# A two-layer graph kernel on Trainium2: a sixth residual-row buffer, a closing norm in four steps, and instructions held to their place

## The chip, the cores and the metric

The kernel runs on one core of one Trainium2 chip. The metric is device time in microseconds (us). Below, PE is the tensor engine (PEld its weight loads), DVE the vector engine, ACT the scalar engine, POOL the GpSimd engine and SP the engine that issues most of the plain DMAs. L1295 is line 1295 of the kernel before.

## The reference, cut to what matters

The input is 32 graphs of 512 nodes with 256 numbers each, and a 0/1 adjacency matrix of each graph. Two layers follow each other. Layer 0 is message passing over the adjacency and a large feed-forward network of sorted (max and min) lines; the change doesn't touch it. Layer 1 is attention over the graph's edges and then a token mixer:

```
attention of one graph, x of 512 x 256:
  h      = layernorm(x) W                      4 heads of 64
  att    = exp(leaky(own + other)) * adjacency, normalised over the neighbours
  v      = relu(att h + bias) + h
  v      = (v - mean) * (var + eps)^-0.5 * gamma + beta     per head: the closing norm
  x      = x + v
mixer of the same graph:
  s      = softmax(layernorm(x) W_slice)       8 heads x 64 slices: "sw"
  tokens = s^T layernorm(x) / sum(s)           "yTp"
  tokens -> gated scan of 64 steps (projection, short convolution, decay matrix, norm)
  x      = x + s (tokens W_out)                "outp"
  out    = x
```

## The kernel before, in words

Layer 1 is `layer1_plain` (L866). It runs two streams over the same engines. The stream `attentions` (L1300) does, graph after graph, `prepare(b + 1)` woven with `attention(b)` and then the closing norm `norm(b, av)`. The stream `mixer(g)` (L1564) takes two graphs at a time (GB = 2, so 16 groups): `slices` for each of them (L1306), `tokens` (L1351), `scan` (L1376) and `unslice` (L1554), which adds outp into x and stores the graph on SP's queue (L1562).

**Order.** Both streams are Python generators. Each `yield n` of the mixer gives the attention stream n times PACE steps to emit; PACE comes from TURNS, STEPS and WANTED, the planned numbers of steps. That decides in which order instructions are handed to the framework's scheduler, which then orders each engine's instructions by priority; `tc.keep_in_program_order` holds one instruction to its handed place. PSUM has four buffers of the kind "any" (hp, lgp, yTp, xp, yp, outp and others) and four of the kind "pv" (avp, adp and the transposes back).

**prepare(b)** (L1135 to 1192) waits, in the planner, until graph b - AHEAD_X is stored, because the tile x has AHEAD_X = 5 buffers. Then POOL gathers the graph's rows by four indirect DMAs (L1142), SP transposes the mask (L1091), POOL issues the narrowing copy of a later mask (`shorten`, L1085). DVE takes the statistics of each row (L1114, 1115), POOL their pow (L31), ACT normalises (L1121), PE transposes (L1130, x3T), and four tiles hp are multiplied on PE (L1171). From each hp tile ACT makes the exponentials hv, mine and other (L1174, 1177, 1178) and the copy ht (L1179), DVE the values hv times the exponential (L1175, read from PSUM). minep (L1183) is the transpose of mine, which goes out to DRAM and comes back broadcast as own (L1187, L1190).

**attention(b)** (L1206): DVE makes the weighed edges att (L1201), PE the sums avp (L1237) and adp (L1242), one row of 16 + 8 matmuls for each of four node tiles; then transposes back (dp, bp, L1220), the division (L1265) and a row of biases added by a DMA (av<-added, L953). `norm` is then put in the list `unfinished` and is stepped from inside the next graph's attention loop.

**norm(b, av)** (L1272): DVE relu and add (L1282), mean (L1284, 1285), subtract (L1286); ACT square (L1288); a first yield; DVE sum of squares (L1290, 1291), POOL pow (L1292), DVE times gamma (L1293); a second yield; DVE times the pow (L1295), DVE add into x (L1296).

**slices** (L1306): statistics d of x, normalise, transpose (x4T), lgp (L1327), ACT exponential (L1328), DVE times a bias factor (L1329), sum, reciprocal and division (L1332 to 1334), PE yTp (L1339) and the transposes swp (L1344). **scan**: xp (L1392), bcp, dtp, zp (L1385), the convolutions on DVE (L1409, 1411), gp (L1479), segp (L1483), qp (L1493), mix (L1500 to 1502), yp (L1509), y (L1512 to 1514), yTp<-ident,y (L1519), oTp (L1527), the mean square msp (L1535), rms on DVE (L1538) and its pow on POOL (L1539), vp (L1549), v (L1551).

Of the kernel before, what the change touches and what calls it, by code (L numbers as in the profile page):

```python
# [13 lines left out]
AF = mybir.ActivationFunctionType  # L14
ALU = mybir.AluOpType
AX = mybir.AxisListType
# [3 lines left out]
P = 128  # L20
N = 512
D = 256
NT = N // P
DC = D // P
LN_EPS = 1e-5
# [839 lines left out]
def layer1_plain(tc, ident, eps, x2s, ranks, adj, w, out, over, ps):  # L865
# [3 lines left out]
    nc = tc.nc  # L869
    B = adj.shape[0]  # L870
    SEG = B // len(x2s)
    GB = 2
    AH, _, HO = w["W"].shape
# [5 lines left out]
    DI = H * C  # L879
# [6 lines left out]
    SLOPE = 0.01  # L886
    HE = HO + 1
    AP = AH // 2
    TURNS = AP * NT + 6
    STEPS = 11  # L890
    WANTED = 68
    AHEAD = 3
    ATT = 2 * (AHEAD + 2) + AP + 1
    HW = P // AH
    AHEAD_X = 2 * GB + 1
    PACE = 1.04 * GB * (TURNS + STEPS) / WANTED

    SMALL = 30.0 * 30.0 / D
# [2 lines left out]
    with ExitStack() as ctx:  # L901
# [11 lines left out]
        def psum(tag, name):  # L913
            return ps.tile([P, N], F32, tag=tag, name=name)
# [36 lines left out]
        def add_rows(dst, i):  # L951

            nc.gpsimd.dma_start(dst, added[i].partition_broadcast(P), accum_op=ALU.add)  # L953
# [44 lines left out]
        with tc.tile_pool(name="raw", bufs=2, side="right") as raw:  # L998
# [67 lines left out]
            for c in range(DC):  # L1066
                sq = raw.tile([P, H * G], F32, tag="wsl2", name=f"wsl2_{c}")
# [68 lines left out]
        def prepare(b):  # L1136

            while b >= AHEAD_X and b - AHEAD_X not in stored:
                yield True
            xt = xs[b] = sb.tile([P, NT, D], F32, tag="x", name=f"x{b}", bufs=AHEAD_X)  # L1140
            for t in range(NT):
                nc.gpsimd.indirect_dma_start(  # L1142
                    out=xt[:, t, :], out_offset=None, in_=x2s[b // SEG],
                    in_offset=bass.IndirectOffsetOnAxis(
                        ap=ranks[:, b * NT + t : b * NT + t + 1].bitcast(U32), axis=0))

            hv = sb.tile([P, NT, AH, HE], F32, tag="hv", name=f"hv{b}")
            xn = hv.rearrange("p t h e -> p (t h e)")[:, : NT * D].rearrange("p (t d) -> p t d", t=NT)
            if b:
                turn(b)  # L1150
            shorten(b + 2)
            yield
            yield
            yield
            normed(xt, xn, f"c{b}")
            add_rows(xt.rearrange("p t d -> p (t d)"), BETA)
            yield
            mask = masked.pop(b)
            xnT = yield from turned(xn, "x3T", f"x3T{b}")
            yield  # L1160


            ht = sb.tile([P, NT, AH * HO], F32, tag="ht", name=f"ht{b}")
            nc.scalar.activation(ht.rearrange("p t e -> p (t e)").bitcast(BF16), mask.rearrange("p t n -> p (t n)"),
                                 AF.Square, bias=centre, accum_out=edges[:, b : b + 1])
            other = sb.tile([P, NT, AH], F32, tag="other", name=f"other{b}")
            mine = sb.tile([P, AH, NT], F32, tag="mine", name=f"mine{b}")
            for t in range(NT):
                ph = psum("any", f"hp{b}_{t}")
                for c in range(DC):  # L1170
                    nc.tensor.matmul(ph[:, : AH * (HO + 2)], xnT[:, c, t * P : (t + 1) * P], wa[:, c, :],  # L1171
                                     start=c == 0, stop=c == DC - 1)
                d = ph[:, AH * HO : AH * HO + AH]
                nc.scalar.activation(hv[:, t, :, HO], d, AF.Exp)  # L1174
                nc.vector.tensor_mul(hv[:, t, :, :HO], ph[:, : AH * HO].rearrange("p (h e) -> p h e", h=AH),  # L1175
                                     hv[:, t, :, HO:].to_broadcast([P, AH, HO]))
                nc.scalar.activation(mine[:, :, t], ph[:, AH * (HO + 1) : AH * (HO + 2)], AF.Exp, scale=1.0 - SLOPE)
                nc.scalar.activation(other[:, t, :], d, AF.Exp, scale=SLOPE - 1.0)
                nc.scalar.copy(ht[:, t, :], ph[:, : AH * HO])  # L1179
                yield  # L1180

            pt = psum("any", f"minep{b}")
            nc.tensor.transpose(pt[: AH * NT, :P], mine.rearrange("p h t -> p (h t)"), ident)  # L1183
            row = sb.tile([AH * NT, P], F32, tag="turned", name=f"turned{b}", bufs=1)
            nc.scalar.copy(row, pt[: AH * NT, :P])
            own_row = dr.tile([AH, N], F32, tag="own", name=f"ownd{b}")
            nc.sync.dma_start(own_row.rearrange("h (t p) -> (h t) p", p=P), row)  # L1187
            own = [wide("own", f"own{b}_{h}", AH + 1) for h in range(AH)]
            for h in range(AH):
                nc.sync.dma_start(own[h], own_row[h].partition_broadcast(P))  # L1190
            ready[b] = mask, ht, hv, other, own
            yield
# [11 lines left out]
        def attention(b):  # L1204

            mask, ht, hv, other, own = ready[b]  # L1206
# [19 lines left out]
            for i, (q, j) in enumerate(turns):  # L1226
                if i + AHEAD < len(turns):
                    begin(b, i + AHEAD)
                elif b + 1 in ready:
                    begin(b + 1, i + AHEAD - len(turns))  # L1230

                if q + 1 == AP:
                    ends = dict(start=j == 0, stop=j == NT - 1)
                    for p in range(AP):
                        for k in range(2 * HO // HW):
                            h, e = 2 * p + k * HW // HO, k * HW % HO
                            nc.tensor.matmul(pv[p][k * HW : (k + 1) * HW, :], hv[:, j, h, e : e + HW],  # L1237
                                             weighed[b, h, j], **ends)
                    if j == 0:
                        pd = psum("pv", f"adp{b}")  # L1240
                    for h in range(AH):
                        nc.tensor.matmul(pd[h * HW : (h + 1) * HW, :], hv[:, j, h, HO:].to_broadcast([P, HW]),  # L1242
                                         weighed.pop((b, h, j)), **ends)
                yield
                if unfinished and i not in (0, 3):
                    next(unfinished[0], None)
                    yield
                    if i > 3:
                        unfinished.pop()
# [12 lines left out]
            for q in range(AP):  # L1262
                bt = back(vT[q], f"bp{q}_")
                heads = slice(2 * q, 2 * q + 2)
# [7 lines left out]
        unfinished = []  # L1272

        def norm(b, av):

            _, ht, _, _, _ = ready[b]
            xt = xs[b]
            NG = NT * AH
            flat = av.rearrange("p t h e -> p (t h e)")
            rows = av.rearrange("p t h e -> p t (h e)")  # L1280
            heads = av.rearrange("p t h e -> p (t h) e")
            nc.vector.scalar_tensor_tensor(flat, flat, 0.0, ht.rearrange("p t e -> p (t e)"), ALU.max, ALU.add)  # L1282
            mu = sb.tile([P, 2, NG], F32, tag="mu", name=f"mu{b}")
            nc.vector.tensor_reduce(mu[:, 0, :], heads, AX.X, ALU.add)  # L1284
            nc.vector.tensor_scalar_mul(mu[:, 0, :], mu[:, 0, :], 1.0 / HO)
            nc.vector.tensor_sub(heads, heads, mu[:, 0, :].unsqueeze(2).to_broadcast([P, NG, HO]))  # L1286
            sq = ht.rearrange("p t (h e) -> p (t h) e", e=HO)
            nc.scalar.activation(sq, heads, AF.Square)  # L1288
            yield
            nc.vector.tensor_reduce(mu[:, 1, :], sq, AX.X, ALU.add)  # L1290
            nc.vector.tensor_scalar(mu[:, 1, :], mu[:, 1, :], 1.0 / HO, 1e-6, ALU.mult, ALU.add)
            nc.gpsimd.tensor_tensor(mu[:, 1, :], mu[:, 1, :], eps[:, 1:2].to_broadcast([P, NG]), ALU.pow)  # L1292
            nc.vector.tensor_mul(rows, rows, gamma.unsqueeze(1).to_broadcast([P, NT, AH * HO]))  # L1293
            yield
            nc.vector.tensor_mul(heads, heads, mu[:, 1, :].unsqueeze(2).to_broadcast([P, NG, HO]))  # L1295
            nc.vector.tensor_add(xt, xt, rows)  # L1296
            del ready[b]
            attended.add(b)

        def attentions():  # L1300
            yield from prepare(0)
            for b in range(B):
                nxt = prepare(b + 1) if b + 1 < B else iter(())
                yield from woven(attention(b), TURNS - 4, nxt, STEPS)
            for _ in unfinished[0]:
# [69 lines left out]
        def scan(g, uT):  # L1375
# [50 lines left out]
            v, e, u, r, dt = (sp[:, i, :] for i in range(5))  # L1426
# [59 lines left out]
            pt = psum("any", f"xtp{g}")  # L1486
# [30 lines left out]
            pt = psum("any", f"yTp{g}")  # L1517
# [14 lines left out]
            pm = psum("any", f"msp{g}")  # L1532
# [2 lines left out]
                    nc.tensor.matmul(pm[i * G : (i + 1) * G, j : j + 1], ident[:, j * G : (j + 1) * G], ms,  # L1535
                                     start=True, stop=True)
            rms = sb.tile([P, GB], F32, tag="rms", name=f"rms{g}")
            nc.vector.tensor_scalar(rms, pm[:, :GB], 1.0 / DI, LN_EPS, ALU.mult, ALU.add)  # L1538
            nc.gpsimd.tensor_tensor(rms, rms, eps[:, 1:2].to_broadcast([P, GB]), ALU.pow)  # L1539
            yield 2  # L1540

# [689 lines left out]
```

## Time and profile before

| what | value |
|---|---|
| runs of the kernel | 4503.5, 4513.17, 4514.52 us (median 4513.17) |
| profiled execution, whole | 4515.02 us |
| its span | 4513.3 us |
| mean granted clock of PE | 0.94 |
| layer 1 within the span | from about 2395 us to the end |
| start of outp in four groups that follow each other | 2715.20, 2844.05, 2973.26, 3102.16 us |
| last stretch, from the 15th group's outp to the end | 124.00 us |

The profile is of one execution. Its page gives busy times of engines over the whole span; the trace can be cut into stretches. A chain of waits is read from the end backwards: each piece is the work that released the next one. A wait is given as engine and line that waited, engine and line that released it, the sum in us, the number of waits and the longest. In a timeline line the bracket at the end is the idle time of that engine before the instruction, and who ended it. "issue" is time for which the trace shows no wait. The granted clock is 1.00 at full speed.

### The profile page before, as it was taken

What the parts mean: (1) busy time and instruction counts of PE and PEld (TensorE: products, weight loads), DVE (VectorE), ACT (ScalarE), POOL (GpSimd) and SP (SyncE); (2) the same over time, 40 slices, a digit from 0 to 9 for tenths busy, and PEclk for the clock granted to TensorE, in tenths of its full rate; (3) what the DMA queues carried; (4) which work ended last, traced back from release to release, by engine and by line L of the source; (5) the groups of instructions that cost most, each with busy time, mean ns of one, the idle gap of its engine ahead of it and who ended that gap; (6) DMA issues with size and microseconds to landing.
All of it is one profiled execution on the core that took longest, in us unless ns stands there. A gap on an engine that the chain in (4) does not pass through costs nothing.

```text
span 4513.3 us, 56135 instructions
## 1 busy us (share of the span) xinstructions
PE 3933.4 (87%) x19799; PEld 2468.0 (55%) x19799; DVE 3204.0 (71%) x6909; ACT 2198.0 (49%) x4305; POOL 1570.2 (35%) x2069
## 2 busy tenths in 40 slices
PE   5567898899988999889997999898998898989987
PEld 4454565656656656555553555555555455555555
DVE  6678888897788877867765766656666666666663
ACT  3345565556565665545663444344444443444433
POOL 2356544664446554444313122222211222222110
PEclk8778999999999999989998999999999999999998
DMA  5546543664446643564315233333322333333210
GB/s 129 160 142 224 184 140 110 206 202 154 135 129 206 194 141 109 169 216 160 129 59 117 52 76 79 80 80 68 83 68 62 73 80 80 80 70 76 62 38 20
DMA packets 301248, 524.04 MB, mean 116 GB/s; under 512 B 104823, under 2 KB 180227, under 8 KB 300956
## 3 DMA queue, kind: packets, MB, share of 16 engines
q0 software_dynamic: 117120, 383.06, 30.6%
q1 hardware_dynamic: 183836, 137.30, 10.4%
q8 instruction: 158, 2.59, 0.2%
q14 instruction: 134, 1.10, 0.1%
HBM read 463.11 MB, written 73.95 MB: 119 GB/s over the span
## 4 chain that ended last, share of the span: by engine, by line
PE 32%; DVE 31%; DMA 15%; issue 9%; POOL 8%; ACT 4%; SPq 1%; DVEq 0%; POOLq 0%; ACTq 0%
DVE acc L637 4%; PE clsp L623 4%; PE po L652 4%; DMA av<-added 3%; PE yTp L1339 3%; PE gatep L623 3%; PE outp L1559 3%; POOL mu L1292 2%; DMA rows<-table,xs 2%; DMA out<-x 2%; DMA rows<-table,tops 2%; DVE best L598 2%; PE oTp L1527 2%; DVE att L1201 2%; PE avp L1237 2%
## 5 line engine op out<-in xcount | busy, mean ns | idle before, releaser
L623 PE MATMUL clsp<-xnT,wc 128*128 128x512 f32 x1024 | 524.8, 631 | 46.7 <-ACT cls L625 34.4
L623 PE MATMUL gatep<-xnT,wg 128*128 128x512 f32 x1024 | 496.8, 605 | 9.3 <-ACT gate L625 9.3
L652 PE MATMUL po<-wd,acc 128*128 128x256 f32 x2048 | 457.3, 382 | 8.4 <-DVE acc L641 5.9
L652 PEld LDWEIGHTS po<-wd,acc 128*128 128x128 f32 x2048 | 389.2, 192 | 75.2 <-issue 9.6
L1201 DVE SCALAR_TENSOR_TENSOR att<-own,other,mask 128x512 f32<-128x512 f32 x512 | 358.3, 737 | 12.8 <-DMA own<-ownd 12.8
L598 DVE SCALAR_TENSOR_TENSOR best<-rows,xs,best 128x1024 f32<-128x1024 f32 x212 | 272.6, 1288 | 126.8 <-ACT best L592 79.5
L637 DVE SCALAR_TENSOR_TENSOR acc<-past,fld,acc 128x512 f32<-128x512 f32 x448 | 344.6, 772 | 23.8 <-ACT past L636 16.0
L1237 PE MATMUL avp<-att,hv 128*32 128x512 f32 x2048 | 333.0, 601 | 7.2 <-DVE att L1201 7.2
L1339 PE MATMUL yTp<-sw,x 128*128 128x512 f32 x512 | 262.1, 666 | 88.0 <-DVE sw L1334 88.0
L623 PEld LDWEIGHTS gatep<-xnT,wg 128*128 128x128 f32 x1024 | 196.8, 196 | 253.3 <-issue 203.5
L632 ACT ACTIVATE acc<-tz,fld 128x512 f32<-128x512 f32 x256 | 198.7, 776 | 279.1 <-PE tz L630 247.4
L636 ACT ACTIVATE past<-tz,fld 128x512 f32<-128x512 f32 x448 | 291.5, 693 | 79.3 <-DVE acc L637 77.7
L595 POOL DMA_INDIRECT rows<-table,xs x212 | 251.5, 1186 | 170.3 <-DVE best L598 117.3
L623 PEld LDWEIGHTS clsp<-xnT,wc 128*128 128x128 f32 x1024 | 183.9, 200 | 185.9 <-issue 114.1
L434 PE MATMUL pm<-h,adj 128*128 128x258 f32 (+1 forms) x1024 | 182.9, 326 | 103.9 <-DVE keep L427 42.6
L1327 PE MATMUL lgp<-wsl,x4T 128*128 128x512 f32 x512 | 241.3, 617 | 22.4 <-ACT x4T L1131 22.4
L625 ACT ACTIVATE gate<-gatep,fld 128x512 f32<-128x512 f32 x256 | 175.4, 685 | 146.4 <-PE gatep L623 124.0
L553 POOL DMA_INDIRECT xs<-rows_of,order x128 | 156.7, 1225 | 215.3 <-DVE acc L637 93.3
L1339 PEld LDWEIGHTS yTp<-sw,x 128*128 128x128 f32 x512 | 104.9, 214 | 227.5 <-DVE sw L1334 126.2
L1559 PE MATMUL outp<-v,swT 128*128 128x256 f32 x1024 | 226.2, 379 | 0.0
L434 PEld LDWEIGHTS pm<-h,adj 128*128 128x128 f32 x1024 | 152.8, 215 | 129.2 <-issue 73.4
L625 ACT ACTIVATE cls<-clsp,fld 128x512 f32<-128x512 f32 x256 | 176.0, 687 | 95.3 <-PE clsp L623 58.8
(593 smaller groups left out, 8550.7 us busy)
## 6 DMA issues: line engine op xcount, KB each, us to landing
adj<-in_adj POOLq DMA_DIRECT2D x128, 256.0 KB
x<-added POOLq DMA_DIRECT2D x64, 512.0 KB
own<-ownd SPq DMA_DIRECT2D x128, 256.0 KB
rows_of<-keep SPq DMA_DIRECT2D x32, 550.0 KB
x<-in_x SPq DMA_DIRECT2D x32, 512.0 KB
x2s<-xs SPq DMA_DIRECT2D x32, 512.0 KB
short<-in_adj POOLq DMA_DIRECT2D x32, 512.0 KB
av<-added POOLq DMA_DIRECT2D x32, 512.0 KB
```

The lines of the kernel that those rows point to most:

```text
L434: nc.tensor.matmul(pm[:, : c1 - c0], a[:, i, t * P : (t + 1) * P], h[:, i, c0:c1], start=i + c0 == 0, stop=i + 1 == NT and c0 > 0)
L595: nc.gpsimd.indirect_dma_start(out=row, out_offset=None, in_=table, in_offset=bass.IndirectOffsetOnAxis(ap=idxs[:, k : k + 1].bitcast(U32) ...
L598: nc.vector.scalar_tensor_tensor(m, row, vals[:, k : k + 1], m, ALU.add, ALU.max)
L623: nc.tensor.matmul(pf, wf[:, c, f * P : (f + 1) * P], xnT[:, c, :], start=c == 0, stop=c == DC - 1)
L625: nc.scalar.activation(o, pf, fn, bias=fld[:, f, bf : bf + 1], scale=1.0 if fn == AF.Gelu else 0.5)
L636: nc.scalar.activation(r, z, AF.Relu, bias=fld[:, f, AT + b : AT + b + 1])
L637: nc.vector.scalar_tensor_tensor(y, r, fld[:, f, CH + b : CH + b + 1], y, ALU.mult, ALU.add)
L652: nc.tensor.matmul(po[:, i, :], acc[f][:, t * P : (t + 1) * P], wd[:, f, :], start=f == 0, stop=f == FC - 1)
L1201: nc.vector.scalar_tensor_tensor(e, own[h], other[:, j, h : h + 1], mask[:, j, :], ALU.max, ALU.mult)
L1237: nc.tensor.matmul(pv[p][k * HW : (k + 1) * HW, :], hv[:, j, h, e : e + HW], weighed[b, h, j], **ends)
L1339: nc.tensor.matmul(py, xn[:, t, c * P : (c + 1) * P], sw[:, t, :], start=t == 0, stop=t == NT - 1)
L1559: nc.tensor.matmul(po[:, :D], swT[:, k, t * P : (t + 1) * P], v[:, k, :], start=k == 0, stop=k == KC - 1)
```

## The change

Six things are edited, all in layer 1.

1. AHEAD_X goes from 5 to 6: one more buffer of the tile x. TURNS goes from 14 to 15 and WANTED from 68 to 69, so that PACE goes from 0.765 to 0.784.
2. In `prepare` the values multiply becomes a function `values(t)`, which reads the copy ht in SBUF in place of the PSUM tile and is handed over one tile later.
3. minep is kept in program order.
4. `unfinished` is stepped at the turns 1, 2, 3 and 6 of the attention loop's eight; before it was stepped at 1, 2 and from 4 on.
5. `norm` has two more yields and so four steps: ahead of the square and ahead of the sum of squares. Its relu, square, sum of squares and the multiply by the pow are kept in program order.
6. In `scan` there is a `yield 1` ahead of rms, and rms is kept in program order.

The narrowing copy was kept in program order already; with the six of the points 3, 5 and 6 that makes seven.

```diff
-    TURNS = AP * NT + 6
+    TURNS = AP * NT + 7
     STEPS = 11
-    WANTED = 68
+    WANTED = 69
...
-    AHEAD_X = 2 * GB + 1
+    AHEAD_X = 2 * GB + 2
...
+            def values(t):
+                nc.vector.tensor_mul(hv[:, t, :, :HO], ht[:, t, :].rearrange("p (h e) -> p h e", h=AH),
+                                     hv[:, t, :, HO:].to_broadcast([P, AH, HO]))
+
             for t in range(NT):
...
                 nc.scalar.activation(hv[:, t, :, HO], d, AF.Exp)
-                nc.vector.tensor_mul(hv[:, t, :, :HO], ph[:, : AH * HO].rearrange("p (h e) -> p h e", h=AH),
-                                     hv[:, t, :, HO:].to_broadcast([P, AH, HO]))
...
                 nc.scalar.copy(ht[:, t, :], ph[:, : AH * HO])
+                if t:
+                    values(t - 1)
                 yield
 
+            values(NT - 1)
+
             pt = psum("any", f"minep{b}")
-            nc.tensor.transpose(pt[: AH * NT, :P], mine.rearrange("p h t -> p (h t)"), ident)
+            tc.keep_in_program_order(
+                nc.tensor.transpose(pt[: AH * NT, :P], mine.rearrange("p h t -> p (h t)"), ident))
...
-                if unfinished and i not in (0, 3):
+                if unfinished and i in (1, 2, 3, 6):
                     next(unfinished[0], None)
...
-            nc.vector.scalar_tensor_tensor(flat, flat, 0.0, ht.rearrange("p t e -> p (t e)"), ALU.max, ALU.add)
+            tc.keep_in_program_order(
+                nc.vector.scalar_tensor_tensor(flat, flat, 0.0, ht.rearrange("p t e -> p (t e)"), ALU.max, ALU.add))
...
-            nc.scalar.activation(sq, heads, AF.Square)
-            yield
-            nc.vector.tensor_reduce(mu[:, 1, :], sq, AX.X, ALU.add)
+            yield
+            tc.keep_in_program_order(nc.scalar.activation(sq, heads, AF.Square))
+            yield
+            tc.keep_in_program_order(nc.vector.tensor_reduce(mu[:, 1, :], sq, AX.X, ALU.add))
...
-            nc.vector.tensor_mul(heads, heads, mu[:, 1, :].unsqueeze(2).to_broadcast([P, NG, HO]))
+            tc.keep_in_program_order(
+                nc.vector.tensor_mul(heads, heads, mu[:, 1, :].unsqueeze(2).to_broadcast([P, NG, HO])))
...
-            nc.vector.tensor_scalar(rms, pm[:, :GB], 1.0 / DI, LN_EPS, ALU.mult, ALU.add)
+            yield 1
+            tc.keep_in_program_order(
+                nc.vector.tensor_scalar(rms, pm[:, :GB], 1.0 / DI, LN_EPS, ALU.mult, ALU.add))
```

## The prediction

> **What bounds the kernel now.** I read the page first, then the busy time by stretches, the waits, the chain of waits and the timeline of one stretch.
>
> ```profile
> PE 3933.4 (87%) x19799; PEld 2468.0 (55%) x19799; DVE 3204.0 (71%) x6909; ACT 2198.0 (49%) x4305; POOL 1570.2 (35%) x2069
> ```
>
> PE is the engine to watch, but 87% is a mean over two layers. The instruction order of layer 0 doesn't change with the edit (PE's orders differ first where layer 1 begins), so I cut layer 1 (2395 us on) at the starts of outp, one stretch for each group of two graphs.
>
> ```profile
> 2844.05:2973.26 129.21, 117.41 (x736) 69.94 (x735) 83.13 (x192) 55.77 (x131) 27.16 (x30) 0.96 0.34 74
> ```
>
> Columns: length, then busy time of PE, PEld, DVE, ACT, POOL, then the granted clock. The stretches repeat (the next is 128.90 with 117.42 of PE): PE idles 11.5 to 11.8 us of 129; some busy time is at a reduced clock too. DVE is busy 83 of 129: it isn't the bound, its order is. The waits of eleven groups (2844 to 4261 us) say who makes PE idle (total, times, longest):
>
> ```profile
> POOL mu L1292 <- DVE mu L1291: 168.2, 11, 15.5
> DVE av L1295 <- POOL mu L1292: 128.1, 22, 9.9
> ...
> PE yTp L1339 <- DVE sw L1334: 73.7, 15, 7.5
> ...
> POOL x L1142 <- DMA out<-x: 51.0, 22, 4.2
> ```
>
> So 73.7/11 = 6.7 us a group are lost ahead of yTp, more than half of PE's idle time. The chain of waits says why:
>
> ```profile
> 2860.96 6.71 DMA out<-x
> ...
> 2873.24 0.61 POOL short L1085
> 2873.85 2.97 POOL mu L1292
> ...
> 2879.53 1.20 DVE sw L1329 x2
> ...
> 2882.81 9.22 PE yTp L1339 x16
> ```
>
> The output store of a finished graph has to land before POOL may gather the next graph into its buffer; the closing norm's pow stands behind that gather on POOL; its multiply (L1295) stands ahead of the softmax of sw on DVE, which sits idle for 8.63 us; PE runs out of work.
>
> **A rule, and the row that bears on it.** The Trainium skill, "TensorE: Matmul & The Clock Gate", section "Part 1: The HAM clock gate (the "warmup" mystery)", says that after an idle window of about 3.4 us PE's clock falls to half and needs a busy window to come back. The trace agrees (the number before PE's is the length, the third from the end the clock):
>
> ```profile
> 2876.00:2880.00 4.00, 0.56 (x3) 0.14 (x1) 3.16 (x4) 0.18 (x1) 1.78 (x2) 1.00 0.79 134
> 2880.00:2884.00 4.00, 1.19 (x2) 0.67 (x3) 4.00 (x10) 0.00 (x0) 0.00 (x0) 0.53 0.35 69
> 2884.00:2888.00 4.00, 4.00 (x7) 1.56 (x6) 4.00 (x10) 0.45 (x3) 0.00 (x0) 0.62 0.00 0
> 2888.00:2892.00 4.00, 4.00 (x12) 1.79 (x11) 2.60 (x15) 0.64 (x2) 1.41 (x3) 1.00 0.00 0
> ```
>
> The 16 yTp matmuls after the stall take 9.22 us; those of each group's second graph take about 7.0. The stall costs 2.2 us besides its own length. I go by the trace's 2.2. The same skill, "DMA: Bandwidth & Descriptors", section "Issuing engines are not separate DMA queues", says that DMAs of different issuers share the same 16 engines; the trace agrees: the first store of a pair landed within 3.24 us, the second, beside gathers and the mask's narrowing copy, after 6.71. So a gather behind a store stays slow whatever engine issues it.
>
> **The change, part by part.** I compared the order of instructions on each engine, before and after.
>
> *Sixth x buffer.* Graph 2g+6 is now gathered where 2g+5 was, still behind a store just issued (its buffer was that of 2g): the POOL wait of 51.0/11 = 4.6 us a group stays. But the rows are needed one graph later. More important, in ten of the groups POOL's pow of the closing norm now comes ahead of the second gather; in three groups in the middle it stays behind.
>
> *Norm in four steps, pinned.* No instruction is added: relu, square, variance sum and the two multiplies cost what they did (1.2 us each on DVE). They move: the multiply by the pow and the add into x come after all four softmax tiles and after the values multiplies (L1175). So nothing of POOL's stands ahead of sw on DVE, but the statistics of the newly gathered graph are mixed in with sw's steps. The row behind is what I can't see; bounds: none of the 6.7 us saved (the statistics wait for the gather in the same place) or all of it. I take 2.0 us of idle time left in the first half, for the chain exp, multiply, sum, reciprocal, multiply of a last tile (some 0.6 us each by the groups).
>
> First half, each of ten groups: idle time 6.25 (yTp) + 1.13 (lgp waiting for x4T) = 7.4 falls to 2.0, **5.4 saved**; half clock, **2.2**; three attention rows were cut in two by other work and now one is. A cut row took 1.0 + 2.7 us and a whole one 3.0, so **1.4**. Sum 9.0.
>
> *Values multiply one tile later, from the copy in SBUF.* ACT's mine no longer waits for DVE's hv (126.3 us of ACT waiting in eleven groups, nearly all covered). On PE minep's 1.30 us goes, but minep now stands directly behind the last hp tile and stays in the scan's own stretch; I keep its 1.3 within the second half's sum below. At layer 1's start minep's 6.2 us wait, which is behind that chain, gets some 3 shorter. The multiply itself reads SBUF, not PSUM: 0.42 us taken as before.
>
> *Scan.* An extra step stands ahead of rms, which holds DVE's rms behind more work; rms waited 7.89 us for PE's msp, covered. Here the first half's gain is paid for, since attention rows and an hp tile that covered the scan's chain moved forward. Before:
>
> ```profile
> 2956.43 1.87 PE L1509 MATMUL yp<-xk,mix 64*64 64x64 f32 x32 [0.64 <-DVE mix L1502]
> 2958.22 1.16 PE L1171 MATMUL hp<-wa,x3T 128*128 128x264 f32 x4
> 2960.68 0.28 PE L1183 MATMUL minep<-ident,mine 128*16 128x128 f32 x1 [1.30 <-ACT mine L1177]
> 2960.79 0.61 PE L1519 MATMUL yTp<-ident,y 128*128 128x128 f32 x4
> 2962.14 5.46 PE L1527 MATMUL oTp<-yT,hoT 128*128 128x128 f32 x32 [0.73 <-ACT yT L1521]
> ```
>
> The scan's idle time is 0.15 (segp) + 0.64 + 1.30 + 0.73 + 0.35 (vp) = 3.2 us. After, yp and the transposes of y have no hp tile between them, and DVE does the moved multiply and add (2.4 us) between mix and y, then two y steps (1.3): 3.8 us against yp's 1.87, so about 2.3 of waiting with the hops. With a row less in front, I put 1.4 ahead of gp, 0.65 at qp and hp, 1.65 at yp (0.64 and one us of lost cover), 0.8 at oTp, 0.35 at vp: 7.15. **Lost: 4.0**, and 0.7 for more of oTp at a low clock (it already takes 5.46 here, 3.84 in the group before). Bounds: nothing lost, or the whole lost cover, one row and one tile (4.2 us), twice over with the clock, some 10.
>
> *SP.* The mask's transpose now stands just ahead of the stores. It waited for attention's last reader of the mask, 30 us before its consumer; I cost it at nothing, since the stores wait for outp later than that; if it were late, the stores and the gathers behind them would be.
>
> **Sum.** Ten groups save 9.0 - 4.7 = 4.3: 43. In four or five of them the row own seems late on DVE and holds rms, so vp: 1.4 each back, 6. Three groups with the old POOL order save 2 each: 6. The start: 3. The last groups, nothing. Together 43 - 6 + 6 + 3 = 46. From the profiled execution (span 4513.3, whole 4515.0) that gives 4469; the median of the runs shown is 1.85 lower, so **4467**.
>
> **The rivals.** *The stall moves (chance 0.14).* The gather still waits for the store, and DVE's statistics of the gathered graph stand between the tiles of sw. Then yTp waits nearly as before and the first half saves 3.6 (1.4 and the clock's 2.2 in a split stall), the second loses 4.7: one us a group worse or a bit better, with the start about 4513. For it: the 4.6 us of POOL waiting stays. Against: an earlier place in time, and sw's first tiles go ahead of it.
>
> *The scan loses its cover (0.18): slower.* Everything PE had to do during conv, mix, y and rms went forward; DVE's moved multiply and add stand within that chain. If the losses there pass 9 us a group the sum turns; at 12, half of it oTp and vp at half clock as after yTp's stall, it is +3 x 14 = 42: 4555. For it: oTp is at 0.77 to 0.80 of the clock there now. Against: DVE has 46 us to spare in a stretch.
>
> *The scan keeps its cover (0.15).* Loss in the second half near nothing: 9 x 13 = 117 less: 4396.
>
> *The forecast (0.53)*, itself from 4440 to 4495.
>
> **How the numbers follow.** About 0.3%, 13.5 us, is what a measurement of this kernel can tell from no change. Faster by more: the forecast, the covered scan, and a little of the moved stall: 0.69. Same: most of the moved stall and the scan's edge: 0.14. Slower: the rest of the scan's case: 0.17. The range takes in the covered scan nearly to its end and half of the slow case: 4400 to 4545.
>
> **What would show it.** Right: DVE's wait for the pow ahead of sw gone, yTp in both graphs at about 7 us, stretches near 124.5 us; PE idle ahead of y's transposes up to 2 us. Wrong: DVE waiting for the gather ahead of sw (the stall moved); scan waits above 9 us a group (slower); a scan without waits (faster still). If layer 0's length changed, the whole comparison would stand on something I haven't seen.

## The result, and the profile after

The changed kernel takes 4528.4 us (median of 9 runs), the kernel before 4510.43 (median of 9): a ratio of 1.0041, 95% interval 1.0028 to 1.0054. It is slower by 0.4%; the prediction was 4467, 1% faster. The profiled execution has a span of 4534.6 us, against 4513.3. (In the table ahead, the first of the four starts of outp is 2716.90 us in the trace, not 2715.20; nothing rests on it.)

I cut it as before, at the starts of outp (length; busy PE, PEld, DVE, ACT, POOL; granted clock; DMA). First the stretch from layer 1's first transpose to the first outp, then two groups, then eleven groups together:

```profile
2400.70:2602.52 201.82, 162.38 (x986) 87.55 (x986) 134.12 (x289) 82.12 (x214) 47.99 (x56) 0.89 0.41 89
2859.08:2986.05 126.97, 117.42 (x737) 69.28 (x734) 84.70 (x193) 56.90 (x134) 28.20 (x30) 0.97 0.35 76
...
3373.88:3508.32 134.44, 122.34 (x737) 71.02 (x734) 83.94 (x193) 54.46 (x130) 29.58 (x30) 0.94 0.32 71
2859.08:4281.55 1422.47, 1306.93 (x8078) 776.54 (x8075) 931.62 (x2113) 612.29 (x1432) 313.72 (x328) 0.96 0.34 73
```

The same cuts before:

```profile
2395.42:2588.78 193.36, 160.10 (x958) 85.14 (x959) 124.92 (x273) 78.31 (x209) 43.23 (x49) 0.88 0.39 87
2843.89:4260.33 1416.44, 1285.81 (x8077) 762.46 (x8075) 913.79 (x2113) 613.49 (x1431) 300.87 (x329) 0.97 0.33 74
```

So the 21.3 us of the two spans are: layer 1's start +8.5; groups 0 to 4 (a group is named by the outp that it starts with) +1.0; groups 5 to 8 +9.9; groups 9 to 12 -3.4; group 13 -2.4; the last two pieces +2.5; and +5.3 before layer 1 begins. The last is not shown to be an effect of the change: layer 0's order is the same in all kernels here, and layer 1 began between 2371 and 2401 us in their profiles.

Over eleven groups PE idles less, (1416.44 - 1285.81)/11 = 11.9 us a group before and (1422.47 - 1306.93)/11 = 10.5 after, but it is busy longer: 116.9 and 118.8. The waits after (total, times, longest) show what the change did:

```profile
DVE stc L1114 <- DMA x<-x2s,ranks: 72.6, 44, 3.4
...
DVE att L1209 <- DMA own<-ownd: 51.9, 35, 4.4
...
PE yTp L1530 <- DVE y L1525: 22.6, 11, 2.3
PE yTp L1350 <- DVE sw L1345: 22.5, 25, 2.4
```

Before, the wait for own was this (it is the broadcast row that attention's att needs):

```profile
DVE att L1201 <- DMA own<-ownd: 3.7, 7, 0.9
```

DVE's wait for the pow ahead of sw is gone; in its place DVE waits 6.6 us a group for the newly gathered rows. It also waits 4.7 us a group for own, where it waited 0.3, and PE waits for y. PE in the scan:

```profile
2956.27 0.41 PE L1490 MATMUL gp<-cpad,bcT 64*64 64x64 f32 x4 [1.23 <-ACT cpad L1465]
...
2960.52 1.06 PE L1504 MATMUL qp<-fcT,xT 128*128 128x8 f32 x8 [0.76 <-ACT ht L1182]
...
2963.85 0.28 PE L1191 MATMUL minep<-ident,mine 128*16 128x128 f32 x1 [0.39 <-ACT mine L1180]
2965.27 1.87 PE L1520 MATMUL yp<-xk,mix 64*64 64x64 f32 x32 [1.14 <-DVE mix L1513]
2969.41 1.09 PE L1530 MATMUL yTp<-ident,y 128*128 128x128 f32 x4 [2.27 <-DVE y L1525]
2971.17 1.65 PE L1538 MATMUL oTp<-yT,hoT 128*128 128x128 f32 x6 [0.67 <-ACT yT L1532]
```

and its clock there, in stretches of 3 us:

```profile
2964.00:2967.00 3.00, 1.86 (x33) 1.76 (x32) 3.00 (x6) 1.20 (x4) 0.91 (x1) 1.00 0.04 8
2967.00:2970.00 3.00, 0.73 (x6) 0.62 (x4) 2.66 (x6) 0.71 (x2) 0.00 (x0) 0.58 1.01 170
2970.00:2973.00 3.00, 2.33 (x11) 1.93 (x10) 1.01 (x2) 2.07 (x5) 0.00 (x0) 0.50 1.01 320
2973.00:2976.00 3.00, 3.00 (x24) 3.00 (x23) 3.00 (x10) 0.00 (x0) 0.00 (x0) 0.79 0.09 34
```

Between 2955 and 2971 us there are six waits, the longest 2.3 us, with narrow matmuls between, and the clock falls to half. It fell at about 2967.5 us (a mean of 0.58 over 3 us is 2.5 us at 0.50), when PE had just begun to wait for y. Until then no wait in this stretch was longer than 1.3 us.

### The profile page after: what moved, and what is told of

Read it like the earlier page. It is cut to its first block, busy times and chain, and to the rows that moved or that the text cites. A ratio compares the mean times of both kernels' runs of the same rounds, so it can differ in the third digit from the quotient of the medians.

```text
span 4534.6 us, 56167 instructions
## 1 busy us (share of the span) xinstructions
PE 3954.2 (87%) x19799; PEld 2479.4 (55%) x19799; DVE 3226.2 (71%) x6909; ACT 2198.7 (48%) x4308; POOL 1584.9 (35%) x2069
## 3 DMA queue, kind: packets, MB, share of 16 engines
q1 hardware_dynamic: 183836, 137.30, 10.8%
## 4 chain that ended last, share of the span: by engine, by line
PE 37%; DVE 23%; DMA 14%; ACT 9%; issue 9%; POOL 7%; SPq 0%; POOLq 0%; another core or an unknown queue 0%; DVEq 0%; ACTq 0%
PE avp L1245 4%; PE yTp L1350 4%; PE clsp L623 4%; DVE acc L637 4%; PE outp L1572 3%; DMA own<-ownd 3%; PE gatep L623 3%; PE po L652 3%; DMA rows<-table,xs 2%; DVE best L598 2%; DMA x<-x2s,ranks 2%; DMA rows<-table,tops 2%; PE adp L1250 2%; POOL x L1142 1%; PE lgp L1338 1%
## 5 line engine op out<-in xcount | busy, mean ns | idle before, releaser
L623 PE MATMUL gatep<-xnT,wg 128*128 128x512 f32 x1024 | 498.0, 606 | 10.5 <-ACT gate L625 9.7
L1350 PE MATMUL yTp<-sw,x 128*128 128x512 f32 x512 | 250.9, 625 | 44.1 <-DVE sw L1345 29.4
L1142 POOL DMA_INDIRECT x<-x2s,ranks x128 | 143.3, 1119 | 205.3 <-DMA out<-x 68.6
```

Source lines behind the costliest of these rows:

```text
L623: nc.tensor.matmul(pf, wf[:, c, f * P : (f + 1) * P], xnT[:, c, :], start=c == 0, stop=c == DC - 1)
L1350: nc.tensor.matmul(py, xn[:, t, c * P : (c + 1) * P], sw[:, t, :], start=t == 0, stop=t == NT - 1)
```

## The experiments

Each run's group mean (groups 2 to 12) is split in three: time lost to the clock (busy time times one minus the granted clock, summed over pieces of 1 us), the rest of PE's busy time, and idle time.

| kernel | ratio to before, interval | group | idle | clock | rest |
|---|---|---|---|---|---|
| before | 1 | 128.8 | 11.9 | 3.3 | 113.6 |
| changed | 1.0041, 1.0028 to 1.0054 | 129.3 | 10.5 | 4.2 | 114.7 |
| e1 late hold on minep | 1.0026, 1.0014 to 1.0039 | 129.1 | 10.6 | 3.8 | 114.6 |
| e2 no new holds | 1.0128, 1.0108 to 1.0148 | 132.8 | 12.3 | 5.5 | 114.9 |
| e3 sixth buffer alone | 0.9940, 0.9920 to 0.9961 | 126.4 | 10.4 | 2.6 | 113.4 |
| e4 changed, old norm | 1.0043, 1.0028 to 1.0057 | 130.3 | 13.0 | 4.5 | 112.8 |
| e5 buffer and norm | 1.0073, 1.0044 to 1.0102 | 131.8 | 10.8 | 7.0 | 114.0 |
| e6 buffer and rms | 1.0027, 1.0017 to 1.0037 | 129.8 | 12.5 | 3.8 | 113.5 |
| e7 buffer and values | 0.9955, 0.9943 to 0.9968 | 127.4 | 12.2 | 2.3 | 112.9 |
| e8 own output tile | 1.0207, 1.0176 to 1.0238 | 135.7 | 14.3 | 5.6 | 115.7 |
| e9 less norm in the scan | 1.0006, 0.9995 to 1.0017 | 129.1 | 9.8 | 4.5 | 114.9 |
| e10 buffer, hold on multiply | 1.0184, 1.0165 to 1.0203 | 133.9 | 15.0 | 5.5 | 113.4 |
| e11 buffer and filling | 0.9962, 0.9941 to 0.9983 | 126.9 | 5.9 | 1.1 | 119.9 |
| e12 late hold, no scan part | 1.0024, 1.0014 to 1.0033 | 129.2 | 10.5 | 4.3 | 114.4 |
| e13 late hold, filling at y | 1.0029, 1.0018 to 1.0039 | 129.2 | 9.6 | 2.8 | 116.8 |
| e14 late hold, filling at yp, y | 1.0021, 1.0004 to 1.0038 | 129.2 | 9.7 | 1.6 | 117.9 |

**e1, the start.** In the changed kernel PE's minep of the second graph, held to its handed place, stands behind the whole attention of the first (2443.16 us, while ACT had mine ready at 2416.2).

```diff
-            tc.keep_in_program_order(
-                nc.tensor.transpose(pt[: AH * NT, :P], ...))
+            turn_mine = nc.tensor.transpose(pt[: AH * NT, :P], ...)
+            if b > 1:
+                tc.keep_in_program_order(turn_mine)
```

> The changed kernel with the hold on minep taken off for the first two graphs only; every other group keeps its order. Theory: in the changed kernel the second graph's minep stands on PE behind the whole attention of the first graph, so own reaches DVE 12 us later (PE's wait at the start 19.8 us against 7.2 before). Then this run loses most of that wait: layer 1's start up to the first outp 201.8 us becomes 190 to 194, the whole some 8 to 10 us below the changed kernel (ratio to before about 1.002). Rival: the start is bounded by POOL's gathers, of which there is one graph more; then the wait only changes its name, the start stays at 200 or more and the time stays at 1.004.

PE's waits in the first 70 us of layer 1, in the changed kernel and then in e1:

```profile
PE avp L1245 <- DVE att L1209: 18.0, 4, 12.9
```

```profile
PE avp L1246 <- DVE att L1210: 11.8, 2, 10.9
```

The start took 195.3 us, 6.5 less than the changed kernel's, somewhat less than expected. In this order the hold is the larger part of the start's loss. The whole times are not clear of each other (1.0026 and 1.0041, with intervals that overlap). 11 us of wait are left where 7.2 were before; the sixth buffer alone has 12.2 too, with one graph's gather more ahead of the first attention. In other orders the start moves by itself: it is 200.0 us in e2 and 202.5 in e5, neither of which has a hold on minep.

**e2, no new holds.** All six are taken off.

> The changed kernel with none of the six new holds (relu, square, sum of squares, multiply by the pow, minep, rms); steps, buffer and values multiply stay. Theory (the holds move DVE's multiply by the pow and add into x between mix and y and so make the scan's waits): the wait ahead of y's transposes falls from 2.1 us a group to under 1, the start loses 8 us as with the late hold, and the stall ahead of yTp stays at some 5 us since two tiles of statistics stand ahead of sw; whole within 0.3% of before, 4500 to 4520. Rival: the holds are what keeps the first stall short, and without them the time is above the changed kernel's, 4535 or more.

The rival was right: 1.0128. The start did not get its 8 us back either (200.0 us). Without the holds the end of the norm and a graph's statistics come ahead of the scan's convolutions on DVE, and gp waits for these. PE's waits in e2:

```profile
PE gp L1487 <- ACT cpad L1462: 46.0, 11, 4.4
PE yTp L1347 <- DVE sw L1342: 37.2, 41, 2.4
```

The wait for y is still 1.6 us a group: the holds don't make it.

**e3, the sixth buffer alone.**

```diff
-    AHEAD_X = 2 * GB + 1
+    AHEAD_X = 2 * GB + 2
```

> The kernel before with the sixth x buffer alone. Theory: POOL's pow still stands behind the second gather and the multiply by it still ahead of sw, so the stall ahead of yTp stays at 6 to 7 us a group: the same as before within 0.3%. Rival: the buffer is what takes the stall away; then yTp waits under 3 us a group and the time is 40 us lower.

Between the theory and the rival: 0.994, the lowest ratio of the study. PE's wait ahead of yTp falls only from 6.7 to 5.15 us a group, DVE waits for the pow as before (125 us in eleven groups), and the group is 2.4 us shorter: 1.5 of idle time, 0.7 of clock.

**e4, the old norm; e5, the norm on the buffer.** e4 takes `norm` and its turns back in the changed kernel; e5 adds them (with TURNS 15 and the four holds) to e3.

> The changed kernel with the norm of before (its yields, the steps at the old turns, no hold in it, TURNS as before); the sixth buffer, the values multiply, minep's and rms's holds stay. Theory: the norm's part makes both the gain ahead of yTp and the loss in the scan; without it the stall ahead of yTp is back at 6 to 7 us and the scan's waits are those of before (under 4 us together), while the start keeps the late minep, 8 to 10 us: 4515 to 4525. Rival: the loss is the norm's alone, and this is at or below before's time.

> The kernel before with the sixth buffer and the norm's part (four steps, steps at turns 1, 2, 3 and 6, TURNS 15, the four holds in it); values multiply, minep and rms as before. The changed kernel and the one with the old norm took the same time, so my theory: the norm's part gives ahead of yTp what it takes in the scan; with the buffer alone at 0.994 of before this is 0.994 within 0.003 (4470 to 4495), yTp waiting 2 to 3 us a group and the scan 6 to 7. Rival: the norm's part pays or costs by itself when the others are gone: under 4465 or over 4500.

e4 came out near what was expected (1.0043): the stall ahead of yTp is back, 6.2 us a group. But the scan waits too, 4.3 us a group where I had given under 4. PE's waits in e4, eleven groups:

```profile
PE yTp L1347 <- DVE sw L1342: 67.7, 28, 5.7
PE yp L1517 <- ACT x L1121: 23.4, 11, 2.1
...
PE vp L1559 <- DVE rms L1548: 10.6, 8, 3.0
```

e5 missed: 1.0073. There the norm's part leaves the idle time as it is in e3 (10.8 and 10.4) but more than doubles the time lost to the clock, 2.6 to 7.0 us. So the norm's part costs by itself. The other parts seem to make up for some of that: e5's interval touches the changed kernel's, but e12 below, which adds the values multiply and the late hold to e5, is clear of it (1.0024).

**e6, the scan's part; e7, the values multiply**, each on e3.

> The kernel before with the sixth buffer and the scan's part alone (one step more ahead of rms, the hold on it, WANTED 69). With the old norm the changed kernel lost 45 us against the buffer alone; its trace shows 2.1 us a group at yp and 1 to 1.5 at vp waiting for rms, which is 3.3 x 14 = 46. Theory: they come from this part, so this run has both waits and takes 4515 to 4530. Rival: the values multiply or minep's hold makes them; then this run is as the buffer alone, 4475 to 4490.

> The kernel before with the sixth buffer and the values multiply from the copy, one tile later, without any new hold. Theory (the scan's part is what costs): as the buffer alone, 4470 to 4490, with minep's wait of 1.3 us a group gone and nothing new at yp. Rival (the values multiply costs): yp waits 2 us a group and the time is 4510 or more.

Both as the theory had it. Against e3, e6 loses 3.4 us a group; vp waits 22.8 us in eleven groups for rms, where e3 has no such wait, and yp 16.9 in place of 7.1. e7 is 0.9955, next to e3's 0.994; minep's wait fell from 1.3 to 0.3 us a group, and vp waits 1.3 us for rms and v.

**e8, the store's chain.** The late hold, five x buffers, and the sum for the output in a tile of its own.

```diff
-                nc.vector.tensor_add(xt[:, t, :], xt[:, t, :], po[:, :D])
-            nc.sync.dma_start(out[b]..., xt)
+                nc.vector.tensor_add(xo[:, t, :], xt[:, t, :], po[:, :D])
+            nc.sync.dma_start(out[b]..., xo)
```

> The changed kernel with the late hold on minep, and with its sixth buffer spent otherwise: five x buffers, and the sum x + outp written to a tile of its own, from which the store reads. So a gather waits for DVE's last add and not for the store to land. Theory: what is left of the stall ahead of yTp (2 to 4 us a group) is DVE's statistics waiting for rows gathered behind the store (72.6 us of DVE waiting in eleven groups); here the wait for the gather falls below 3 us a group, yTp's below 1.5, and the time is some 20 us under the late hold's 4514. Rival: the gather isn't what ends last there (ACT's exponentials and DVE's own work are); then yTp waits as before and the time is 4514 or more, since graphs are gathered one later.

My theory failed: 1.0207. DVE waits 82.6 us for gathered rows, more than the changed kernel's 72.6. With five buffers a graph is gathered one later, and its statistics are needed at once. As two things changed, it doesn't tell what the store's chain is worth; that stays open.

**e9, less of the norm in the scan.** Work is left out, as the expectation says.

```diff
+            n, k = (NG, NT) if b % 2 else (2, 1)
-                nc.vector.tensor_mul(heads, heads, mu[:, 1, :]...)
-            nc.vector.tensor_add(xt, xt, rows)
+                nc.vector.tensor_mul(heads[:, :n], heads[:, :n], mu[:, 1, :n]...)
+            nc.vector.tensor_add(xt[:, :k], xt[:, :k], rows[:, :k])
```

> The changed kernel with the late hold on minep, but for even graphs (whose norm ends inside the scan, between mix and y) the multiply by the pow is done on an eighth of the elements and the add into x on a quarter: work is left out there, so that DVE spends some 0.5 us between mix and y instead of 2.4. The order of the instructions on DVE and PE stays nearly the same. Theory: the short waits of the scan are paid twice, as idle time and in PE's clock. Then the wait ahead of y's transposes (2.2 us a group) falls to about 0.3, the time lost to the clock from 3.8 us a group to 2.5 or less, and a group is 3 us or more shorter: 42 us or more under the late hold, 4475 or less. Rival: only the wait goes (1.9 us a group, 4488), or the next wait takes its place (4505 or more).

The theory failed. The wait for y fell from 2.2 to 1.6 us only, and the clock's share rose (3.8 to 4.5). The multiply and the add were not what y waits for in the main: yp's end and two DVE steps are.

**e10, one hold only**, on the multiply by the pow, on top of e3.

> The kernel before with the sixth buffer and one hold only, on the closing norm's multiply by the pow; all steps as before. DVE then does sw ahead of the multiply, two tiles of statistics of the newly gathered graph still ahead of sw; PE's order is that of the buffer alone (four cut rows, the scan's cover in place). Theory: DVE's wait for the pow ahead of sw goes (11 us a group in the buffer alone), what ends last there is then the gather, so yTp waits 3 to 4 us instead of 5.2; in the scan the multiply and add stand ahead of y and cost about 1.5 us: together 4470 to 4485, as the buffer alone. Rival: the hold gives the whole first stall back while the scan stays covered: under 4455.

Both were wrong: 1.0184. With two tiles of statistics of the gathered graph ahead of sw, the stall ahead of yTp is larger than in any other run. Waits of PE and DVE in eleven groups of e10:

```profile
PE yTp L1340 <- DVE sw L1335: 98.7, 29, 7.6
...
DVE shiftc L1119 <- POOL rsc L31: 68.7, 22, 5.9
...
DVE stc L1114 <- DMA x<-x2s,ranks: 34.0, 7, 6.1
```

This is the mechanism of my first rival, in a kernel that shows it fully: the statistics of the gathered graph take the closing norm's place ahead of sw. DVE waits for that graph's rows (stc) and, longer, for POOL's pow of its variance (shiftc).

**e11, PE kept busy in the stall**, on top of e3.

```diff
                 py = psum("any", f"yTp{b}_{c}")
+                if j == 0 and c == 0:
+                    for _ in range(8):
+                        nc.tensor.matmul(py, ident, wsl[:, 0, :], start=True, stop=True)
```

> The kernel before with the sixth buffer, and eight extra matmuls (ident by the slice weights, 128x512) in each group, issued ahead of the first graph's yTp into its own PSUM tile, which yTp then overwrites. They add 8 x 0.43 = 3.4 us of PE work inside an idle time of 5.2 us and change no other order. Theory: the idle time costs its length and the clock after it; with PE kept busy yTp runs at the full clock, time lost to the clock falls from 2.6 us a group to about 1, and the whole by 1.5 x 15 = 20 us or more against the buffer alone: 4440 to 4462. Rival: the half clock after the wait is covered by something that ends later (DVE's sw, swT), or the extra matmuls push yTp: 4480 or more.

The clock came back and the time didn't change. Each extra call is two matmul instructions, so they took 7.0 us and not 3.4. PE's timeline in e3: the hp ahead of the stall, yTp at half clock, and swp:

```profile
2995.04 1.16 PE L1171 MATMUL hp<-wa,x3T 128*128 128x264 f32 x4
3001.09 9.25 PE L1339 MATMUL yTp<-sw,x 128*128 128x512 f32 x16 [4.89 <-DVE sw L1334]
3010.17 1.91 PE L1344 MATMUL swp<-ident,sw 128*128 128x128 f32 x16
```

In e11, with the filling, at the full clock (the same view):

```profile
2991.31 7.03 PE L1340 MATMUL yTp<-wsl,ident 128*128 128x512 f32 x16
2998.18 1.88 PE L1342 MATMUL yTp<-sw,x 128*128 128x512 f32 x4
3001.05 5.42 PE L1342 MATMUL yTp<-sw,x 128*128 128x512 f32 x12 [1.00 <-DVE sw L1334]
3006.31 1.91 PE L1347 MATMUL swp<-ident,sw 128*128 128x128 f32 x16
```

DVE's multiply by the pow, from which the chain runs, started at 2996.58 in e3 and 2992.72 in e11. To swp that is 13.59 us in both, and 13.6 to 13.7 in eight of the eleven groups of each. So yTp's stage goes at the pace of DVE's sw tiles, and the half clock there costs next to nothing.

**e12, without the scan's part**, on top of e1.

> The changed kernel with the late hold on minep and without the scan's part (no step ahead of rms, no hold on it, WANTED 68 again). Added to the sixth buffer alone, the scan's part cost 3.4 us a group. Theory: parts of this change don't add up, since each moves the whole order: with the norm's part in place rms hardly waits (under 0.1 us a group), so taking the step out doesn't give 3.4 us back; attention rows land elsewhere, and the run is at 4510 or more, between the late hold (1.0026) and sixth buffer with norm (1.0073). Rival: the scan's part costs here what it costs alone; then 4470 or less.

1.0024, as the late hold's 1.0026; the rival's 4470 is out. What costs 3.4 us a group next to the buffer alone costs nothing next to the norm's part.

**e13 and e14, PE kept busy in the scan**, on top of e1.

```diff
             pt = psum("any", f"yTp{g}")
+            for _ in range(2):
+                nc.tensor.matmul(pt, ident, wsl[:, 0, :], start=True, stop=True)
```

> The changed kernel with the late hold on minep, and two extra matmul calls (four matmul instructions of 512 columns, some 1.8 us at the full clock) between yp and y's transposes, into the PSUM tile that the transposes then overwrite; the order of everything else is the same. They lie in PE's wait for y (2.2 us a group). Theory: the half clock over y's transposes, oTp and the transposes back lies on the path (nothing else is late there); with PE busy in the wait the time lost to the clock falls from 3.8 us a group to 2.5 or less and a group gets 1 to 2 us shorter: 14 to 28 us under the late hold's 1.0026 of before, that is 0.996 to 0.999. Rival: the chain of DVE and ACT bounds the scan as DVE bounded yTp's stage; the clock comes back and the time stays at 1.002 to 1.004.

> As the run before it, with one extra call ahead of yp and two around it (one of them lands ahead of yp too, one ahead of y's transposes): 1.8 us of extra work in yp's wait of 1.2 us and 0.9 us in y's. Theory: the clock doesn't fall at all in the scan; lost to the clock 2 us a group or less, but yp comes some 0.6 us later; 0.995 to 1.000. Rival: yp is on the chain that bounds the scan, so its delay is paid in full: 1.004 or more.

(e14 has one more such call ahead of yp.) e13's time is its rival's, 1.0029. e14's 1.0021 lies between its theory and its rival, though its clock came back (1.6 us a group lost). What that was worth is seen in the stretch from y's transposes to outp, as a mean of groups 2 to 12:

| kernel | from y's transposes to outp | lost to the clock there | vp waits for rms and v | from minep to outp |
|---|---|---|---|---|
| e1 | 17.0 | 2.7 | 0.3 | 22.6 |
| e13 | 16.1 | 0.8 | 1.2 | 22.7 |
| e14 | 17.0 | 0.6 | 1.9 | 22.6 |

In e13 2.0 us of clock come back and the stretch is 0.8 shorter; but most of its extra matmuls met the low clock (2.9 us a group; 1.8 at the full clock), and y's transposes start 0.8 us later. In e14 2.1 us come back and the stretch is as long as it was: the time turns up as waits of vp. Waits in eleven groups of e14:

```profile
DVE att L1210 <- DMA own<-ownd: 50.3, 31, 4.0
...
PE vp L1566 <- ACT v L1568: 11.3, 11, 1.1
PE vp L1566 <- DVE rms L1555: 10.1, 9, 2.3
```

On DVE rms stands behind attention's att, and att waits for own, about 4.6 us a group in both and in e1. own is made from minep, and from minep to outp the three kernels take the same time, whatever the clock. So the low clock over the scan lies, for the most part, beside the chain of own; 0.8 us a group is the most that these runs show it to cost.

## Why the prediction was wrong

**The idle time came out right, in part by luck.** Forecast for ten groups: 5.4 us saved, 4.0 lost, -1.4; measured -1.4, as a mean of eleven groups, the others among them. Two misses cancel in it. yTp and lgp kept 3.5 us (forecast 2.0), so that 4.5 were saved; the scan waits 6.4 (forecast 7.15), so that 3.3 were lost: gp 1.04, qp 0.72, minep 0.55, yp 1.07, y 2.06, oTp 0.67, vp 0.30. The wait for y has about the size forecast (2.3), but only in part its cause: with most of the multiply and the add left out it is still 1.6 (e9).

**The step that failed is "half clock, 2.2"**, with the 0.7 set against it: 1.5 us a group less were to be lost to the clock, and it was 0.9 more. First, it was no time to be had. That yTp took 9.22 us where the second graph's takes 7.0 I put down to the clock, but DVE delivers sw at that pace (e11). In the changed kernel yTp runs at the full clock and still takes 8.8 us from its first matmul to swp (timeline of PE):

```profile
2890.12 3.49 PE L1350 MATMUL yTp<-sw,x 128*128 128x512 f32 x6
2894.47 4.56 PE L1350 MATMUL yTp<-sw,x 128*128 128x512 f32 x10 [0.87 <-DVE sw L1345]
2898.87 1.91 PE L1355 MATMUL swp<-ident,sw 128*128 128x128 f32 x16
```

Second, the low clock moved into the scan. By parts of a group (the first 64 us and what is left), time lost to the clock went from 2.4 and 0.9 us to 1.0 and 3.2. The Trainium skill, "TensorE: Matmul & The Clock Gate", section "Part 1: The HAM clock gate (the "warmup" mystery)", speaks of an idle window of about 3.4 us; here the clock fell after waits of at most 1.3 us that came close together, while I had priced the scan's waits by their length alone. But of this loss, too, the runs show at most 0.8 us a group as paid (e13, e14).

**What the scan's end follows is own**, which the forecast has as late in four or five groups, 6 us in all. In the changed kernel a row of the next graph's attention (24 matmuls in most groups) stands between gp and outp, where none stood before. So DVE needs own earlier, and waits for it 4.7 us a group in place of 0.3. As means, from outp to gp 105.8 us became 99.0, and from gp to the next outp 23.0 became 30.3; 3.0 of these 7.3 are more work of PE there, at the full clock. From minep to outp it is 22.5 us, as in e1, e13 and e14. This is read from the traces: no run brought own earlier.

**"Cut rows, 1.4" failed too.** Busy time apart from the clock rose by 1.1 us a group. I had counted the first half alone; over the whole group there are four cuts before and five after in most groups, and matmuls of yTp spaced by DVE count as busy. The size was off as well: in the trace before, a whole row takes 2.8 us (the forecast has 3.0) and a cut one 1.0 and 2.8, so one cut is worth 1.0 and not 0.7. Attention's rows take 1.0 us a group more, which is one cut, and yTp 0.8.

**The start**, forecast -3, was +8.5. I had looked at whom the second graph's minep no longer waits for, not at what its hold puts it behind. e1 has 6.5 less.

**Groups 5 to 8**, forecast to gain 6 by the three with the old POOL order, lost 9.9. In groups 6 to 8 one wait of 4.1 to 5.2 us of yTp for sw's exponentials is left in each. The clock's loss in the first 64 us is 1.7 to 3.5 us in groups 5 to 8; of the other seven groups only one has any (1.7). The scan's clock loss is no mark of them: 2.0 to 4.1 us here, 2.1 to 3.9 in the others. Which part of the change makes these orders wasn't tried.

Of the sum (46 us less forecast, 21.3 more in the profile), the groups make 48 of the difference, the start 11.5, and what lies outside the forecast (before layer 1 and the end) 7.8. Of the rivals, the first (the gather ahead of sw) is half there, 6.6 us a group of DVE waiting, and shown whole in e10. The slower one (the scan loses its cover) has the right place, but the scan lost about 3.3 us of waits and 2.3 of clock, most of the latter not paid, and not the 9 that I set as its point. The point was lower because the gain was: 4.5 us of waiting, not 9.0. Of the signs of being right, two came (no wait for the pow ahead of sw, 2.1 us ahead of y's transposes) and two did not (the first graph's yTp in 8.8 us and not 7, stretches of 129.3 and not 124.5).

What stays open: what an earlier own would give, what the store's chain alone is worth, and what e5's loss to the clock costs. Where e5 loses it can be seen: 4.2 us a group from gp on (e3 0.8), and 2.8 ahead of that, where PE waits 3.0 to 3.3 us for ACT's x ahead of one x4T in every group, which it doesn't in e3.

## What to carry to other kernels

Before a low clock is counted as a gain to be had, look at what feeds that stage: if the operand tiles come at the pace of another engine, the slow matmuls lie beside it. Several short waits can bring the low clock as one long wait does. Whether it is paid can be tried by filling the waits: here the clock came back in two stages, and the time hardly did. Then look at what the other engines wait for: DVE's wait for own was on the first list of waits, and told more of the scan than the clock did. A hold that fits the steady order has to be read at the start of the loop too; and of a change with many parts, try each alone: here one line (the sixth buffer) gave 0.6% and the rest took 1%.

## What the runs showed of the hardware

PE's granted clock fell to 0.50 although no wait of the 12 us before was longer than 1.3 us; in the 3 us that ended half a microsecond earlier PE had been busy 1.86 us, nearly all with matmuls of 64x64. In float32 a matmul call of 512 columns shows as two matmul instructions in the trace: 8 calls were 16 instructions and 7.03 us.
